# Two streams of other work beside a recurrent scan, on one Trainium2 core

## The chip, the cores and the metric

The kernel runs on one core of a Trainium2 chip. The core has a matrix engine (TensorE, in the profile PE, with PEld for its weight loads), VectorE (DVE), ScalarE (ACT), GpSimd (POOL) and SyncE (SP), which mostly issues transfers. Each engine works through its own queue in order. The metric is the device time of one execution in microseconds. The time before is 11773.53 us, the median of 3 runs (11760.24 to 11794.41).

## The reference, cut to what matters

The model is four layers on four images of 96 channels and 64 x 64 pixels.

```python
# layer 0: norms, 3x3 convolution, then a selective scan in four directions k over 4096 pixels,
#          192 channels x 16 states, then output norm, gate and projection
def step(h, inp):
    d_t, u_t, b_t, c_t = inp
    dA = jnp.exp(d_t[..., None] * A)                             # the decay, da
    h = dA * h + (d_t * u_t)[..., None] * b_t[:, :, None, :]      # inflow db, recurrence hh
    y = jnp.einsum('bkdn,bkn->bkd', h, c_t)                       # hc, then summed over the states
    return (h, y)
...
x = x + _L0_conv_ref(_gn(x), ...)      # layer 0
x = x + _L1_conv_ref(_gn(x), ...)      # layer 1: deformable 3x3 convolution: 9 gathered samples a pixel
t = t + _L2_attn_ref(_ln_t(t), ...)    # layers 2-3, on tokens: a Fourier block,
t = t + _L2_ffn_ref(_ln_t(t), ...)     #   a feed-forward block with fp8 rounding,
t = t + _L3_attn_ref(_ln_t(t), ...)    #   linear attention,
t = t + _L3_ffn_ref(_ln_t(t), ...)     #   and another feed-forward block
```

Images are independent of each other. Within an image the layers follow each other.

## The kernel before

The scan of layer 0 is cut into 1536 units: 4 images x 4 directions x 4 stretches of 1024 pixels x 24 groups of 8 channels with 16 states each, which fill 128 rows. A unit is a pipeline over the engines (loads of `da`, `du` and others in `fetch`, then one stage for each engine):

```python
def fetch(self, u, before):                     # cut
    u.da = sp.tile([128, T], F32, name=f"da{u.key}", tag="da", bufs=5)
    nc.sync.dma_start(u.da, src.unsqueeze(0).to_broadcast([NS, D8, T]))
def decay(self, u):    # ScalarE
    nc.scalar.activation(u.da, u.da, AF.Exp, scale=self.al[:, a : a + 1])
def inflow(self, u):   # TensorE: two matmuls into PSUM, db
def recur(self, u):    # VectorE
    nc.vector.tensor_mul(u.db, u.db, u.bc[:, 0, :])
    nc.vector.tensor_tensor_scan(hh, da, db, first, ALU.mult, ALU.add)
def weigh(self, u):    # GpSimd
    u.hc = self.sp.tile([128, T], F32, name=f"hc{u.key}", tag="hc", bufs=4)
    nc.gpsimd.tensor_mul(u.hc, u.hh, u.bc[:, 1, :])
def total(self, u, v): # TensorE sums hc over the states into py; settle (ScalarE) and store (SyncE) follow
```

All other work is a generator that yields its steps with an estimated cost on each of four engines. Between two units the kernel takes steps until one engine's share of a unit is spent. A pause costs nothing, and there is one stream only:

```python
SHARE = cost(5.0, 1.9, 4.5, 3.3)       # PE, DVE, ACT, POOL: us of other work per unit

def others():
    yield from l0.before(0)            # preparation of image 0
    for b in range(B):
        if b:
            yield from l1.image(b - 1)
        if b + 1 < B:
            yield from l0.before(b + 1)
        if b:
            yield from l23.image(b - 1)
        yield from l0.behind(b)        # output projection
    yield from l1.image(B - 1)
    yield from l23.image(B - 1)
...
for _, goes in l0.scan():
    if not goes:
        next(work)
        continue
    room = [min(r + s, SAVED * s) for r, s in zip(room, SHARE)]
    while min(room) > 0:
        step = next(work, None)
        if step is None:
            break
        room = [r - s for r, s in zip(room, step)]
```

The weighted sums of layer 1, for 128 pixels, run in three pieces of three taps:

```python
for k0 in (0, 3, 6):
    nc.vector.tensor_mul(g4, g4, w4.unsqueeze(2).to_broadcast([128, 12, C]))
    nc.vector.tensor_add(s1, s1, g[:, ks, 2 * C :])
    nc.vector.tensor_add(s2, s1[:, :, :C], s1[:, :, C:])
```

Of the kernel before, what the change touches and what calls it, by code (L numbers as in the profile page):

```python
# [20 lines left out]
L = H * W  # L21
# [21 lines left out]
def prepare(x, **w):  # L43
# [84 lines left out]
    a["selb"] = np.broadcast_to(eye8[:, :, None], (8, 8, 128)).copy()  # L128
# [37 lines left out]
SHARE = cost(5.0, 1.9, 4.5, 3.3)  # L166
SAVED = 1.5

# [28 lines left out]
def pause(rounds):  # L197
    for _ in range(rounds):
        yield NOTHING


class Net:
# [3 lines left out]
    def __init__(self, ctx, tc, ins):  # L206
# [5 lines left out]
        for name in ("vecs", "ident", "cen96", "grp3", "selv", "selb"):  # L212
            setattr(self, name, self.load(name, self.const))
# [7 lines left out]
        nc.vector.memset(self.one, 1.0)  # L221
        self.exp_and_log()

# [99 lines left out]
    def spread(self, rstd, j, n, key):  # L323

        k = rstd.shape[0]
        pb = self.mm(f"lnb{key}_{j}", n)
        self.nc.tensor.matmul(pb, lhsT=self.selb[:k, j, :n], rhs=rstd, start=True, stop=True)
        return pb
# [24 lines left out]
class Layer0:  # L353
# [45 lines left out]
    def before(self, b):  # L399
        net = self.net  # L400
        tc, nc, ins = net.tc, net.nc, net.ins
        with tc.tile_pool(name=f"l0u{b}", bufs=1) as up:
# [3 lines left out]
            with tc.tile_pool(name=f"l0b{b}", bufs=1) as sm:  # L406
# [4 lines left out]
                order = [(0, j) for j in range(NT)] + [(1, j) for j in reversed(range(NT))]  # L411
                xdbl = {}

                def chains():
                    yield self.projected(b, *order[0], us, xp_a, xp_c, sm, xdbl)
                    for n, (pr, j) in enumerate(order):
                        for t in range(3):
                            yield self.steps(b, pr, j, t, us, dtw, sm, xdbl)
                            if t == 0 and n + 1 < len(order):
                                yield self.projected(b, *order[n + 1], us, xp_a, xp_c, sm, xdbl)  # L420
# [3 lines left out]
    def inputs(self, b, up, us):  # L424

        net = self.net
        tc, nc, ins = net.tc, net.nc, net.ins
# [3 lines left out]
        with tc.tile_pool(name=f"l0a{b}", bufs=1) as big, tc.tile_pool(name=f"l0i{b}", bufs=2) as sm:  # L431
            x = big.tile([C, L], F32, name=f"xg{b}", tag="t1")
            nc.sync.dma_start(x, ins["x"][b])
            wc = big.tile([C, 9, 256], F32, name=f"wc{b}", tag="wc")
            nc.sync.dma_start(wc, self.wc_d)
            wz = big.tile([C, DI], F32, name=f"wz{b}", tag="wz")
            nc.sync.dma_start(wz, ins["w_in"][:, 256:])
            pad = big.tile([C, PW, PW], F32, name=f"pad{b}", tag="pad")
            for edge in (pad[:, 0, :], pad[:, PW - 1, :], pad[:, :, 0], pad[:, :, PW - 1]):
                nc.gpsimd.memset(edge, 0.0)  # L440
# [14 lines left out]
            def rows(j):  # L455
                return pad[:, 1 + j * NR : 1 + (j + 1) * NR, 1 : 1 + W]

            def as_rows(t):
                return t.rearrange("p (h w) -> p h w", w=W)

            yield from net.centred(x, cen, lambda j: (rows(j), as_rows), f"0_{b}", sm, bias)
            rs = net.rstd

            def normed_rows(j):
                pb = net.spread(rs, j, C, f"0_{b}")
                yield cost(pe=0.9)
                nc.vector.tensor_mul(rows(j), rows(j), as_rows(pb))
                yield cost(dve=0.7)
                nc.scalar.activation(
                    rows(j), rows(j), AF.Identity, scale=net.vec(V_ING, C), bias=net.vec(V_INB, C)  # L470
                )
                yield cost(act=0.8)

            yield from pipe((normed_rows(j) for j in range(NCH)), 3)
            xct_v = xc.rearrange("p (w h) -> p h w", h=H)

            def convolved(j):
# [28 lines left out]
                for g, (c0, n) in enumerate(((0, 128), (128, D2))):  # L506
                    pz = net.mm(f"pz{g}_{b}_{j}", n)
                    nc.tensor.matmul(pz, lhsT=wz[:, c0 : c0 + n], rhs=rows(j), start=True, stop=True)
# [11 lines left out]
            yield from pipe((convolved(j) for j in range(NCH)), 2, every=7)  # L520

    def projected(self, b, pr, j, us, xp_a, xp_c, sm, xdbl):
# [3 lines left out]
        nc = net.nc  # L526
        for q in range(2):
            k = 2 * pr + q
            xd = sm.tile([NX, T], F32, name=f"xd{b}_{k}_{j}", tag=f"xd{q}", bufs=2)
            hp = slice(64 * q, 64 * q + 64)  # L530
            for h in range(T // CH):
                t0 = j * T + h * CH
                ua = us[0][:, t0 : t0 + CH] if q == 0 else us[1][:, t0 // H : (t0 + CH) // H, :]
                px = net.mm(f"px{b}_{k}_{j}{h}", NX)
                nc.tensor.matmul(px, lhsT=xp_a[:, k, :], rhs=ua, start=True, stop=False)
                nc.tensor.matmul(
                    px, lhsT=xp_c[hp, pr, :], rhs=us[2][hp, t0 : t0 + CH], start=False, stop=True
                )
                nc.scalar.activation(xd[:, h * CH : (h + 1) * CH], px, AF.Identity, bias=net.vec(V_X1, NX))  # L539
                yield cost(pe=1.7, act=0.7)  # L540
            xdbl[pr, j, q] = xd
        for q in range(2):
            nc.sync.dma_start(
                self.bc_d[b][2 * pr + q][:, j * T : (j + 1) * T], xdbl[pr, j, q][: 2 * NS]
            )
        yield NOTHING

    def steps(self, b, pr, j, t, us, dtw, sm, xdbl):
# [3 lines left out]
        ts = slice(j * T, (j + 1) * T)  # L552
        tk = f"{b}_{pr}_{j}_{t}"

        def tile_of(name, bufs):
            return sm.tile([128, T], F32, name=f"{name}{tk}", tag=name, bufs=bufs)



        rl, ex = tile_of("rl", 2), tile_of("ex", 3)  # L560
        for h in range(T // CH):
            hs = slice(h * CH, (h + 1) * CH)
            pd = net.mm(f"pd{tk}_{h}")
            for q in (0, 1) if t == 2 else (t,):
                o, m = (pd[64 * q : 64 * q + 64], slice(128, DI)) if t == 2 else (pd, slice(0, 128))
                nc.tensor.matmul(  # L566
                    o,
                    lhsT=dtw[2 * NS :, 2 * pr + q, m],
                    rhs=xdbl[pr, j, q][2 * NS :, hs],
                    start=True,  # L570
                    stop=True,
                )
            nc.scalar.activation(rl[:, hs], pd, AF.Relu)
            nc.scalar.activation(ex[:, hs], pd, AF.Abs)
            yield cost(pe=1.9 if t == 2 else 0.95, act=1.2)
        nc.scalar.activation(ex, ex, AF.Exp, scale=-1.0)
        lw, w1 = tile_of("lw", 2), tile_of("w1", 2)
        nc.scalar.activation(lw, ex, AF.Ln, bias=net.one)  # L578
        nc.scalar.activation(w1, ex, AF.Identity, bias=net.one)
        yield cost(act=3.3)  # L580
        nc.vector.tensor_add(rl, rl, lw)  # L581
        nc.vector.scalar_tensor_tensor(w1, w1, -1.0, ex, ALU.add, ALU.subtract)
        yield cost(dve=3.2)
        nc.vector.tensor_sub(rl, rl, w1)  # L584
        yield cost(dve=1.3)
        if t == 1:
            u = us[1][:, j * T // H : (j + 1) * T // H, :]
            nc.gpsimd.tensor_mul(
                ex.rearrange("p (w h) -> p w h", h=H), rl.rearrange("p (w h) -> p w h", h=H), u
            )  # L590
        else:
            nc.gpsimd.tensor_mul(ex, rl, us[t][:, ts])  # L592
        parts = ((0, 128, 2 * pr + t, 0),) if t < 2 else ((0, 64, 2 * pr, 128), (64, 128, 2 * pr + 1, 128))
        for p0, p1, k, c0 in parts:
            nc.sync.dma_start(self.de_d[b][k][c0 : c0 + p1 - p0, ts], rl[p0:p1])
        yield cost(pool=2.4)
        du = sm.tile([128, 3, T], BF16, name=f"du{tk}", tag="du", bufs=2)
        nc.scalar.copy(du[:, 0, :], ex)
        yield cost(act=1.1)
        nc.gpsimd.tensor_sub(ex, ex, du[:, 0, :])  # L600
        yield cost(pool=2.4)
        nc.scalar.copy(du[:, 1, :], ex)
        yield cost(act=1.1)
        nc.vector.tensor_sub(du[:, 2, :], ex, du[:, 1, :])
        yield cost(dve=1.6)
        for p0, p1, k, c0 in parts:
            dst = self.du_d[b][k][:, c0 : c0 + p1 - p0, ts]
# [5 lines left out]
    def scan(self):  # L613
# [13 lines left out]
        for n in range(len(units) + 5):  # L627
            while loaded < min(n + ahead + 1, len(units)):
                u = units[loaded]
                while (u.b, u.k // 2, u.j) not in self.ready:  # L630
                    yield u.b, False
# [28 lines left out]
            yield at(min(n, len(units) - 1)).b, True  # L660
# [776 lines left out]
```

## Time and profile before

| | kernel before |
|---|---|
| time, median of 3 | 11773.53 us |
| head, to the first recurrence | 460 us |
| scan, first to last recurrence | 10002 us |
| tail | 1281 us |
| VectorE busy in the scan | 7575 us, so 2427 us idle |
| granted TensorE clock, mean | 0.672 |

The prediction below shows the busy line, the stages and several groups. Two further views matter for the comparison. The first is VectorE's row of the page's 40 slices, where each digit is the busy share in tenths, 9 being 90% or more:

```profile
DVE  0484888877997587754799668675489977534411
```

The second lists what ended VectorE's idle time within the scan (460 to 10462 us). In lists of waits, after the colon stand the total in us, the number of waits and the longest.

```profile
DVE db L716 <- PE db L705: 1160.7, 175, 34.0
DVE du L604 <- ACT du L602: 149.2, 43, 8.5
...
DVE nw L259 <- ACT nw L257: 114.5, 7, 20.3
...
DVE rl L581 <- ACT lw L578: 65.9, 43, 3.8
```

The 4s, 5s and 6s in the middle of the row lie in the scan, which VectorE should carry. Nearly half of the idle time there is one wait: 175 times the multiply `db` stood for a matmul that came late, by 6.6 us on average and by up to 34.0 us. TensorE was busy for 6359.67 of the scan's 10002 us, so it was not short of time on the whole. The longest of these waits, which ends at 5383 us, can be followed in the trace: TensorE stood 25.5 us in front of a matmul of output projection that waited for GpSimd's `ya`, and the matmul for `db` lay behind it in the same queue. The other waits were not followed one by one.

### The profile page before, as it was taken

What the parts mean: (1) busy time and instruction counts of PE and PEld (TensorE: products, weight loads), DVE (VectorE), ACT (ScalarE), POOL (GpSimd) and SP (SyncE); (2) the same over time, 40 slices, a digit from 0 to 9 for tenths busy, and PEclk for the clock granted to TensorE, in tenths of its full rate; (3) what the DMA queues carried; (4) which work ended last, traced back from release to release, by engine and by line L of the source; (5) the groups of instructions that cost most, each with busy time, mean ns of one, the idle gap of its engine ahead of it and who ended that gap; (6) DMA issues with size and microseconds to landing.
All of it is one profiled execution on the core that took longest, in us unless ns stands there. A gap on an engine that the chain in (4) does not pass through costs nothing. (4 is left out here: it accounts for less than half of the span.)

```text
span 11743.4 us, 86182 instructions
## 1 busy us (share of the span) xinstructions
PE 7376.3 (63%) x28728; PEld 2510.8 (21%) x28728; DVE 7989.7 (68%) x5552; ACT 4209.3 (36%) x6446; POOL 6050.7 (52%) x3212
## 2 busy tenths in 40 slices
PE   4758655565445866876554676687654468754486
PEld 1102000011111202521111120352111135212262
DVE  0484888877997587754799668675489977534411
ACT  2555543332222653343222365334322223431123
POOL 0362665655885464434688446443468844345601
PEclk9657655566555856876655675686665578766685
DMA  1354557766665455634666555552476656334410
GB/s 37 113 167 110 168 165 183 178 152 157 172 177 130 136 169 144 162 81 128 160 173 177 126 140 163 144 154 78 124 176 177 179 139 159 87 100 115 120 41 6
DMA packets 618302, 1605.21 MB, mean 137 GB/s; under 512 B 142185, under 2 KB 159165, under 8 KB 614978
## 3 DMA queue, kind: packets, MB, share of 16 engines
q1 hardware_dynamic: 544130, 1373.13, 44.4%
q0 software_dynamic: 73728, 226.57, 7.1%
q8 instruction: 229, 3.75, 0.1%
q14 instruction: 215, 1.76, 0.1%
HBM read 1343.11 MB, written 256.29 MB: 136 GB/s over the span
## 5 line engine op out<-in xcount | busy, mean ns | idle before, releaser
L730 POOL TENSOR_TENSOR hc<-hh,bc 128x1024 f32<-128x1024 f32 x1536 | 3927.2, 2557 | 3536.2 <-DVE hh L719 3053.3
L719 DVE TENSOR_TENSOR_SCAN hh<-da,st,db 128x1024 f32<-128x1024 f32 x1152 | 2703.5, 2347 | 194.6 <-ACT st L726 53.6
L705 PE MATMUL db<-du,rep 96*128 96x512 bf16 x3072 | 1356.7, 537 | 2136.8 <-DVE hh L719 1965.8
L716 DVE TENSOR_TENSOR db<-db,bc 128x1024 f32<-128x1024 f32 x1536 | 1872.2, 1219 | 1178.4 <-PE db L705 1178.3
L700 ACT ACTIVATE da<-da,w_al 128x1024 f32<-128x1024 f32 x1536 | 1758.0, 1149 | 1154.5 <-DMA da<-de 1091.4
L1018 POOL DMA_INDIRECT g<-table,idx x1152 | 1312.9, 1140 | 401.0 <-issue 352.4
L747 PE MATMUL py<-hc,w_fold 128*32 128x512 f32 x6144 | 1290.8, 915 | 15.2 <-POOL hc L730 15.2
L705 PEld LDWEIGHTS <-rep 96*128 96x128 bf16 x3072 | 238.9, 111 | 3346.3 <-DVE hh L719 2690.9
L719 DVE TENSOR_TENSOR_SCAN hh<-da,db 128x1024 f32<-128x1024 f32 x384 | 878.2, 2287 | 74.7 <-ACT da L700 20.6
L1046 PE MATMUL ps<-w_ident,s 128*96 128x128 f32 x1152 | 298.0, 390 | 985.9 <-DVE s L1042 981.6
L1047 ACT COPY st<-ps 96x384 f32<-96x384 f32 x384 | 182.2, 475 | 1853.2 <-PE ps L1046 1764.5
L1037 DVE TENSOR_TENSOR g<-g,wt 128x1152 f32<-128x1152 f32 x384 | 533.0, 1388 | 152.8 <-DMA g<-table,idx 152.8
L726 ACT COPY st<-hh 128x1 f32<-128x1 f32 x1152 | 212.0, 184 | 926.4 <-DVE hh L719 922.3
L484 PE MATMUL pc<-pad,wc 96*128 96x512 f32 x1152 | 516.2, 603 | 0.4
L1042 DVE TENSOR_TENSOR s<-g 128x288 f32<-128x288 f32 x384 | 438.0, 1141 | 18.8
L1046 PEld LDWEIGHTS ps<-w_ident,s 128*96 128x96 f32 x1152 | 156.8, 170 | 1326.4 <-issue 681.8
L1040 DVE TENSOR_TENSOR g<-g 128x576 f32<-128x576 f32 x384 | 394.8, 1028 | 5.8
L1053 PE MATMUL pd<-st,wdc 96*96 96x256 f32 x1152 | 397.9, 511 | 0.0
L581 DVE TENSOR_TENSOR rl<-rl,lw 128x1024 f32<-128x1024 f32 x96 | 221.8, 2311 | 244.3 <-ACT lw L578 243.3
L566 PE MATMUL pd<-xd,dtw 7*64 7x512 f32 (+1 forms) x512 | 315.0, 929 | 1.6 <-ACT xd L539 0.9
L747 PEld LDWEIGHTS py<-hc,w_fold 128*32 128x32 f32 x6144 | 171.2, 136 | 639.5 <-issue 564.7
L592 POOL TENSOR_TENSOR ex<-rl,xa 128x1024 f32<-128x1024 f32 x32 | 78.7, 2459 | 434.1 <-DVE rl L584 434.1
(240 smaller groups left out, 9776.0 us busy)
## 6 DMA issues: line engine op xcount, KB each, us to landing
da<-de SPq DMA_DIRECT2D x1536, 512.0 KB
du<-du SPq DMA_DIRECT2D x384, 192.0 KB
bc<-bcd SPq DMA_DIRECT2D x128, 512.0 KB
du<-du SPq DMA_DIRECT2D x64, 768.0 KB
y<-yb SPq DMA_DIRECT2D x384, 128.0 KB
de<-rl SPq DMA_DIRECT2D x64, 512.0 KB
m<-in_dft SPq DMA_DIRECT2D x128, 256.0 KB
du<-du SPq DMA_DIRECT2D x64, 384.0 KB
```

Source lines behind the costliest of these rows:

```text
L484: nc.tensor.matmul(pp, lhsT=wc[:, q, g * 128 : (g + 1) * 128], rhs=pad[:, r0 + dy : r0 + dy + NR, dx : dx + W], start=(q == 0), stop=(q == 8),
L700: self.net.nc.scalar.activation(u.da, u.da, AF.Exp, scale=self.al[:, a : a + 1])
L705: self.net.nc.tensor.matmul(db[:, h, :], lhsT=self.rep[:96, u.s % 4, :], rhs=u.du[u.s // 4][:, h * CH : (h + 1) * CH], start=True, stop=True,)
L716: nc.vector.tensor_mul(u.db, u.db, u.bc[:, 0, :])
L719: nc.vector.tensor_tensor_scan(u.along(u.hh), u.along(u.da), u.along(u.db), first, ALU.mult, ALU.add)
L730: self.net.nc.gpsimd.tensor_mul(u.hc, u.hh, u.bc[:, 1, :])
L747: nc.tensor.matmul(py[p0 : p0 + 32], lhsT=self.fold[:, u.i, :], rhs=hc[:, h * CH : (h + 1) * CH], start=u.add is None and u.i == 0, stop=( ...
L1018: nc.gpsimd.indirect_dma_start(out=g[:, k, :], out_offset=None, in_=self.tables[b % 2], in_offset=bass.IndirectOffsetOnAxis(ap=idx[:, 9 * ...
L1037: nc.vector.tensor_mul(g4, g4, w4.unsqueeze(2).to_broadcast([128, 12, C]))
L1042: nc.vector.tensor_add(s2, s1[:, :, :C], s1[:, :, C:])
L1046: nc.tensor.transpose(pt[:, k, :], s2[:, k, :], net.ident)
L1053: nc.tensor.matmul(po, lhsT=wdc[:, k, :], rhs=st[:, k, :], start=(k == 0), stop=(k == 8))
```

## The change

The intent is to run two streams of other work beside the scan instead of one after the other. One has preparation of all images and layers 2-3, the other has output projection and layer 1. Each stream earns a number of steps per unit, and pauses cost whole units, so the chains are spread. Room for the second stream is made by smaller pieces and fewer buffers. The scan's loads move from SyncE's queue to ScalarE's. The core of the diff, with cuts marked:

```diff
-SHARE = cost(5.0, 1.9, 4.5, 3.3)
+SHARE = cost(4.5, 2.0, 3.6, 3.0)
+LAG = tuple(0.5 * s for s in SHARE)
...
-def pause(rounds):
-    for _ in range(rounds):
-        yield NOTHING
+def pause(units):
+    for _ in range(units):
+        yield SHARE
...
# steps of preparation: half tiles (128 x 512), lw and w1 in one buffer, one operation moved to GpSimd
-        rl, ex = tile_of("rl", 2), tile_of("ex", 3)
...
-        lw, w1 = tile_of("lw", 2), tile_of("w1", 2)
+        lw, w1 = tile_of("lw", 1), tile_of("w1", 1)
...
-        nc.vector.scalar_tensor_tensor(w1, w1, -1.0, ex, ALU.add, ALU.subtract)
+        nc.vector.scalar_tensor_tensor(rl, pd, 0.0, lw, ALU.max, ALU.add)
+        nc.gpsimd.tensor_sub(w1, w1, ex)
...
# fetch: bc, du, add, da
-                nc.sync.dma_start(...)
+                nc.scalar.dma_start(...)
...
-        u.hc = self.sp.tile([128, T], F32, name=f"hc{u.key}", tag="hc", bufs=4)
+        u.hc = self.sp.tile([128, T], F32, name=f"hc{u.key}", tag="hc", bufs=3)
...
# output projection: blocks of two tiles instead of four, half of y at a time, fewer load buffers
-        HB = 4
+        HB = 2
...
# layer 1: whole-tile sums, two gather buffers
-                g = gp.tile([128, 9, 4 * C], F32, name=f"g{key}", tag="g", bufs=3)
+                g = gp.tile([128, 9, 4 * C], F32, name=f"g{key}", tag="g", bufs=2)
...
-                for k0 in (0, 3, 6):
...
+                nc.vector.tensor_mul(g4, g4, w4.unsqueeze(2).to_broadcast([128, 36, C]))
+                yield cost(dve=4.0)
...
-        def others():
...
+        def ends():
+            yield from l0.before(0)
+            l23 = Layers23(ctx, net, x2, out)
+            yield from l23.prepare()          # was in the head
+            yield from l0.before(1)
+            yield from l0.before(2)
+            yield from l0.before(3)
+            for b in range(B):
+                yield from l23.image(b)
+
+        def middle():
+            yield from l1.cleared()           # was in the head
+            for b in range(B):
+                yield from l0.behind(b)
+                yield from l1.image(b)
+
+        streams = [Stream(ends(), 2.6), Stream(middle(), 1.9)]
...
+            for stream in streams:
+                stream.credit = min(stream.credit + stream.earns, 3.0)
+            while go():                       # takes steps while there is credit and room
+                pass
+        while not all(stream.over for stream in streams):     # after the scan: alternately
```

## The prediction

> **What bounds the kernel now.** A scan of 1536 units is the spine: each unit is one multiply (`db`) and one recurrence (`hh`) on VectorE, one decay on ScalarE, one multiply on GpSimd. All other work (preparation of an image "before" its scan, output projection "behind" it, layer 1, layers 2-3) is emitted between units into the same in-order queues. I first read the page's busy line, then split the span where `hh` starts and ends: it runs from 460.0 to 10462.4 us. So: head 460, scan 10002, tail 1281 us. Next I cut these into stages by busy time per stretch.
>
> ```profile
> PE 7376.3 (63%) x28728; PEld 2510.8 (21%) x28728; DVE 7989.7 (68%) x5552; ACT 4209.3 (36%) x6446; POOL 6050.7 (52%) x3212
> ```
> ```profile
> core 0: us, PE busy (x) PEld busy (x) DVE busy (x) ACT busy (x) POOL busy (x), PEclk, DMA share, GB/s
> 0.00:156.00 156.00, 0.00 (x0) 0.00 (x0) 11.82 (x40) 4.41 (x10) 0.79 (x8) 1.00 0.19 53
> ...
> 1758.00:2313.00 555.00, 292.77 (x1008) 39.89 (x1008) 496.85 (x289) 190.00 (x280) 339.56 (x144) 0.56 0.73 183
> ...
> 2900.00:3513.00 613.00, 299.67 (x1026) 103.07 (x1026) 594.50 (x408) 150.31 (x249) 502.18 (x301) 0.58 0.66 174
> ...
> 5129.00:5568.00 439.00, 300.70 (x717) 78.62 (x716) 219.06 (x183) 158.47 (x290) 170.67 (x101) 0.67 0.41 108
> 10462.00:11107.00 645.00, 290.36 (x868) 136.84 (x864) 278.00 (x352) 82.50 (x162) 365.80 (x318) 0.65 0.42 114
> 11107.00:11743.00 636.00, 469.40 (x3028) 268.84 (x3028) 85.47 (x121) 179.25 (x334) 39.34 (x34) 0.70 0.09 25
> ```
> The same stretches for `hh` alone give the units in each (the count beside DVE):
> ```profile
> 1758.00:2313.00 555.00, 334.94 (x145) 21.69 (x118) 339.56 (x144) 0.56 0.73 183
> 2900.00:3513.00 613.00, 223.91 (x97) 13.42 (x72) 271.02 (x96) 0.58 0.66 174
> ...
> 5129.00:5568.00 439.00, 111.61 (x49) 8.64 (x47) 110.32 (x47) 0.67 0.41 108
> ```
> Three regimes. In 1758-2313 nothing runs beside the scan, and a unit costs 555/145 = 3.83 us, near VectorE's own 1.22 + 2.33 = 3.55. In 2900-3513 (layer 1's sampling) VectorE is 97% busy at 613/97 = 6.3 us. In 5129-5568 (end of layers 2-3, then output projection of image 1) a unit costs 439/49 = 9.0 us with no engine above 70%: that is waiting. It comes from chains emitted too densely and from SyncE's queue:
> ```profile
> SPq L696 <- DVE hh L719: 5594.0, 1128, 22.9
> ```
> ```profile
> DVE db L716 <- PE db L705: 104.7, 13, 34.0
> ...
> POOL ya L803 <- DMA ya<-y: 55.6, 5, 25.8
> ```
> The first line (the DMA queue's own waits, whole span) says SyncE stands half the span in the wait of the scan's `da` load for a scan to free its buffer; every other load queues behind it. The other two (chain of waits, 5129-5568): a late `ya` load stops GpSimd, then TensorE, whose in-order queue then brings `db` up to 34 us late to VectorE. VectorE's busy time within the scan is 7989.7 - 50.9 (head) - 363.5 (tail) = 7575 us of 10002, so 2427 us of the scan is VectorE idle.
>
> **What the Trainium skill says.** "SBUF — State Buffer", Who interferes with whom: a VectorE instruction with two SBUF inputs contends with a GpSimd instruction that reads SBUF, and the later one blocks fully. The trace agrees: the sum `s<-g` costs three times as much beside the scan (2900-3513) as in the tail (10700-11000), while the recurrence, with one SBUF and one PSUM input, never moves from 2347 ns.
> ```profile
> L1042 DVE TENSOR_TENSOR s<-g 128x288 f32<-128x288 f32 x68 | 94.5, 1390 | 2.4
> ```
> ```profile
> L1042 DVE TENSOR_TENSOR s<-g 128x288 f32<-128x288 f32 x67 | 30.7, 458 | 6.2
> ```
> "DMA: Bandwidth & Descriptors", Issuing engines are not separate DMA queues: transfers issued from different engines share the 16 DMA engines, and only the issuer's sequencer time is saved. So I expect no bandwidth from ScalarE's queue; what it buys is that other loads no longer stand behind a wait. An issue is not free:
> ```profile
> L696 SPq DMA_DIRECT2D da<-de x1536: 514/515/4586, 443.7 to 10444.4; - x192
> L581 DVE TENSOR_TENSOR rl<-rl,lw x96: 1210/2433/3429, 395.2 to 7375.9; 128x1024 f32<-128x1024 f32 x96
> ```
>
> **The change part by part.**
>
> *Head.* Before, table clearing holds SyncE from 16.5 to 113.6 us (16 stores, about 6 us apart), then weights of layers 2-3 are prepared until 156; only then the first group norm starts, and 304 us later the scan. Both now run beside the scan. I estimate the first image loaded by about 30 us, so 30 + 304 = 335: saves 125.
>
> *VectorE in the scan.* Sampling: per tile three times (1388 + 1028 + 1141) = 10.7 us become one triple over all nine taps. Uncontended cost (tail stretch) is 3 x (1356 + 758 + 458) = 7.7; three waits for the shared port, not nine, about 0.45 each on average: 9.0. Over the 96 tiles in the scan: -160 us. Preparation: four two-tile 128x1024 operations of 2311 + 1775 + 1799 + 1917 ns, 24 per image, = 187 us, become 48 x (0.70 reading PSUM + 1.15 + 1.15) = 144; one went to GpSimd (48 x 1.25). Over four images -170. Half of output projection moves from tail into the scan, three quarters of layers 2-3 of image 2 move the other way (-65). I get about 7290 us for the scan's VectorE, 4.75 us a unit.
>
> *ScalarE.* 1536 + 384 + 288 + 128 = 2336 issues at about 0.55 us: +1280 us, 0.84 a unit. With decay (1.15), state copy and other work I count 3.0 to 5.5 us a unit: below VectorE except in preparation, where they are close. The issue waits for `hh` of the unit before, which the state copy just after it did anyway.
>
> *Order and pace.* This is the main part. The queues' order shows, by unit: preparation of image 0 to unit 95, of 1 at 120-243, 2 at 251-382, 3 at 390-608; layer 1 of image 0 at 412-715; then per image output projection over 70 units (was 13), sampling over 209 (was 134), layers 2-3 over 303 beside them. The 150 units that ran alone are filled. To price it, I summed for every 24 units what stands in each queue, each kind at its mean from this trace, and took the larger of VectorE and TensorE:
> units 0-96: 4.85 us a unit; 96-168: 5.38; 168-264: 5.14; 264-288 (convolution, TensorE): 7.16; 288-408: 5.14; 408-456 (TensorE): 6.56; 456-720: 5.23; 720-912: 4.60; 912-1104: 5.18; 1104-1296: 4.60; 1296-1488: 5.18; to 1536: 5.28. Sum 7837.
> The same sum over the kernel before gives 8677 where 10002 were measured: a factor 1.153, which is 1.04 in sampling, 1.06 in the bare scan, and 1.3 to 1.46 where output projection or the end of layers 2-3 was squeezed into a dozen units. Those squeezed stretches are gone, since a pause now costs whole units and a stream takes 2.6 or 1.9 steps a unit. I choose 1.15 for the preparation stretch (2449 us of the sum, ScalarE near its limit) and 1.09 for the rest (5388): 2816 + 5873 = 8690.
>
> *Tail.* Before: 645 for output projection and layer 1 of image 3, 636 for layers 2-3. At the end of the scan the new order still has one and a half halves of the Fourier block and the rest of layers 2-3 of image 2 (about 500 us alone). It goes step for step beside layer 1 of image 3, but its last block spills over (about 60). TensorE has some 240 + 265 us there in alternating order, so I take 720 instead of 645 (less one half of output projection, more mutual waiting). 720 + 60 + 640 = 1420, a loss of 140.
>
> Sum: 335 + 8690 + 1420 = 10445, say 10450.
>
> **Rivals.**
> 1. DMA becomes the bound. Its engines' share is 51.6% of the span, of which some 5650 us fall in the scan; in 8690 that is 65%, and the bare scan ran at 73% share and 183 GB/s with ScalarE waiting for `da` 98 times (296.6 us). For: output projection now reads half columns in 128-byte pieces. Against: VectorE was 90% busy at that share. If bursts at block starts hurt: scan 9200, total 11000.
> 2. ScalarE's queue becomes the clock: a late decay delays the next issue, which delays the next decay. For: 4.8-5.5 us a unit in preparation. Against: it has two units between issue and need. It would cost 0.5 us on 600 units, 300 us: 10750.
> 3. Three PSUM buffers and two gather buffers shared by two streams tie them together, TensorE waits for an eviction and `db` comes late as before. Then the factor stays 1.15: scan 9035, total 10800.
> 4. Smoothing works fully (factor 1.05): 8230, total 9950.
> 5. The spilled layers 2-3 simply add to the tail: 1700, total 10700.
>
> **Range and chances.** The scan's factor dominates: 1.05 to 1.18 is 8230 to 9250, and the tail adds +-120. Range 9900 to 11100. Being within 2% of 11774 needs a scan above 9780, a factor of 1.25, which only the squeezed stretches had. Faster 0.93, same 0.05, slower 0.02.
>
> **What will show it.** First `hh` near 335; last near 9030; tail near 1420 with sampling stretched. No stretch of bare scan at 3.8 us before unit 1500; units at 5.2-5.6 us in sampling with VectorE over 90%; VectorE's idle time waiting for `db` well below the 1178 us of before; `ya` no longer late. Wrong would be: ScalarE idle on `da` above 1500 us, VectorE below 80% in units 456-1488, or a DMA share above 80%.

## The result

The changed kernel takes 10492.59 us, the median of 4 runs (10462.69 to 10508.04). The kernel before took 11783.97 us in the same rounds. The ratio is 0.8903, with a 95% interval of 0.8877 to 0.8929. A ratio here is the mean time of one kernel's runs over the mean of the other's in the same rounds, so it is not quite the ratio of the medians quoted. Executions over 1.5% slower than the fastest of the same kernel are left out of the means. Where kernels of different rounds are compared below, I take the difference of their ratios times 11,770 us.

| | before | predicted | after |
|---|---|---|---|
| time | 11773.53 | 10450 | 10492.59 |
| head | 460 | 335 | 323 |
| scan | 10002 | 8690 | 8676 |
| of it units 0-456 | | 2816 | 2853 |
| of it units 456-1536 | | 5873 | 5823 |
| tail | 1281 | 1420 | 1462 |
| VectorE busy in the scan | 7575 | 7290 | 7201 |
| VectorE idle in the scan | 2427 | | 1475 |
| granted TensorE clock, mean | 0.672 | | 0.702 |

The busy line of the changed kernel's page and its row for VectorE:

```profile
PE 7119.7 (68%) x28728; PEld 2481.0 (24%) x28728; DVE 7640.0 (73%) x4993; ACT 4352.7 (42%) x6950; POOL 6456.3 (62%) x3603
...
DVE  0788688587759999987878889788888897444211
```

The stages of the changed kernel, by busy time in each stretch:

```profile
core 0: us, PE busy (x) PEld busy (x) DVE busy (x) ACT busy (x) POOL busy (x), PEclk, DMA share, GB/s
0.00:323.00 323.00, 229.84 (x422) 75.50 (x422) 41.48 (x61) 145.34 (x175) 26.44 (x29) 0.88 0.22 62
323.00:3153.00 2830.00, 2029.64 (x5220) 447.99 (x5220) 2117.23 (x1475) 1604.91 (x2400) 1685.63 (x933) 0.68 0.61 160
3153.00:4650.00 1497.00, 804.41 (x2654) 199.79 (x2654) 1405.94 (x804) 586.57 (x939) 1228.27 (x693) 0.64 0.70 183
4650.00:5616.00 966.00, 742.01 (x4242) 324.10 (x4243) 789.50 (x521) 356.52 (x580) 554.62 (x268) 0.75 0.72 177
5616.00:6685.00 1069.00, 653.88 (x2311) 214.89 (x2309) 944.49 (x548) 393.76 (x668) 891.55 (x483) 0.68 0.68 174
8999.00:10461.00 1462.00, 1055.68 (x6192) 609.15 (x6188) 397.52 (x367) 412.72 (x787) 474.00 (x376) 0.73 0.25 69
```

The bare stretch at 3.8 us a unit is gone, and so are the squeezed ones at 9. The fastest 48 units take 4.20 us each, the slowest 7.01. In 3153-4650 (sampling of image 0, 268 units at 5.59 us) VectorE is 94% busy, and in 5616-6685 (sampling of image 1 beside layers 2-3, 192 units at 5.57 us) 88%. In the preparation stretch, 323-3153, it is 75% busy, so waits are left there. The granted clock rose as well; whether as a cause or as a consequence, no run tells.

VectorE's waits within the scan (323 to 8999 us), and two of SyncE's own waits over the whole span:

```profile
DVE db L741 <- PE db L730: 574.4, 178, 22.0
DVE rl L604 <- ACT lw L599: 137.4, 57, 17.3
DVE g L1085 <- DMA g<-table,idx: 85.3, 35, 6.7
```
```profile
SPq L789 <- ACT yb L782: 1976.3, 130, 33.4
...
SPq L619 <- DVE rl L607: 984.8, 180, 18.3
```

The wait of `db` for its matmul has halved, 1160.7 to 574.4 us, at nearly the same number of waits: each became shorter. That is 586 of the 952 us that VectorE's idle time fell by. SyncE no longer stands in front of the loads of `da`, but it now stands in front of the store of `y` (L789) and of the store of `de` (L619) instead.

The rows that answer to those of the sums, of preparation's first operation and of the `da` load:

```profile
L1085 DVE TENSOR_TENSOR g<-g,wt 128x3456 f32<-128x3456 f32 x128 | 593.1, 4634 | 148.6 <-DMA g<-table,idx 147.3 <-issue 1.2
...
L1088 DVE TENSOR_TENSOR g<-g 128x1728 f32<-128x1728 f32 x128 | 261.4, 2042 | 1.0
...
L1091 DVE TENSOR_TENSOR s<-g 128x864 f32<-128x864 f32 x128 | 153.3, 1197 | 1.7
L604 DVE SCALAR_TENSOR_TENSOR rl<-pd,lw 128x512 f32<-128x512 f32 x192 | 130.7, 681 | 309.6 <-ACT lw L599 309.5
```
```profile
L721 ACTq DMA_DIRECT2D da<-de x1536: 521/522/1621, 306.4 to 8973.7; - x192
```

The three sums of a tile are now (593.1 + 261.4 + 153.3) / 128 = 7.87 us, against 10.67 before, as a mean over all 128 tiles. For the 96 tiles within the scan it is 8.21 against 11.65. The prediction expected 9.0 for these, coming from 10.7, which is the mean over all tiles.

### The profile page after: what moved, and what is told of

It reads as the page before. It is cut to its first block, busy times and chain, and to the rows that moved or that the text cites. A ratio compares the mean times of both kernels' runs of the same rounds, so it can differ in the third digit from the quotient of the medians.

```text
span 10460.6 us, 85850 instructions
## 1 busy us (share of the span) xinstructions
PE 7119.7 (68%) x28728; PEld 2481.0 (24%) x28728; DVE 7640.0 (73%) x4993; ACT 4352.7 (42%) x6950; POOL 6456.3 (62%) x3603
## 5 line engine op out<-in xcount | busy, mean ns | idle before, releaser
L755 POOL TENSOR_TENSOR hc<-hh,bc 128x1024 f32<-128x1024 f32 x1536 | 3885.8, 2531 | 1937.3 <-DVE hh L744 1003.6
L725 ACT ACTIVATE da<-da,w_al 128x1024 f32<-128x1024 f32 x1536 | 1762.6, 1149 | 3126.4 <-DMA da<-de 981.5
L730 PE MATMUL db<-du,rep 96*128 96x512 bf16 x3072 | 1293.0, 515 | 2324.6 <-DVE hh L744 2147.1
L1074 POOL DMA_INDIRECT g<-table,idx x1152 | 1449.7, 1258 | 417.2 <-issue 191.1
L1085 DVE TENSOR_TENSOR g<-g,wt 128x3456 f32<-128x3456 f32 x128 | 593.1, 4634 | 148.6 <-DMA g<-table,idx 147.3
L605 POOL TENSOR_TENSOR w<-w,ex 128x512 f32<-128x512 f32 x192 | 259.0, 1349 | 650.7 <-ACT w L601 648.9
L607 DVE TENSOR_TENSOR rl<-rl,w 128x512 f32<-128x512 f32 x192 | 304.9, 1588 | 95.6 <-POOL w L605 95.3
L1332 POOL CAST xqf<-fl 96x512 fp8e5<-96x512 f32 x64 | 51.5, 810 | 496.6 <-DVE fl L1291 496.5
L604 DVE SCALAR_TENSOR_TENSOR rl<-pd,lw 128x512 f32<-128x512 f32 x192 | 130.7, 681 | 309.6 <-ACT lw L599 309.5
L592 PE MATMUL pd<-xd,dtw 7*128 7x512 f32 (+1 forms) x512 | 324.5, 953 | 43.9 <-ACT xd L570 28.5
L1109 PE MATMUL pd<-st,wdc 96*96 96x256 f32 x1152 | 309.0, 414 | 0.0
L518 PEld LDWEIGHTS pc<-pad,wc 96*128 96x128 f32 x1152 | 220.5, 195 | 310.5 <-issue 290.4
L628 DVE TENSOR_TENSOR du<-ex,du 128x512 bf16<-128x512 f32 x192 | 234.6, 1222 | 79.7 <-ACT du L626 75.3
```

What stands on the lines that cost most here:

```text
L518: nc.tensor.matmul(pp, lhsT=wc[:, q, g * 128 : (g + 1) * 128], rhs=pad[:, r0 + dy : r0 + dy + NR, dx : dx + W], start=(q == 0), stop=(q == 8),
L592: nc.tensor.matmul(o, lhsT=dtw[2 * NS :, 2 * pr + q, m], rhs=xdbl[pr, j, q][2 * NS :], start=True, stop=True)
L607: nc.vector.tensor_sub(rl, rl, w1)
L725: self.net.nc.scalar.activation(u.da, u.da, AF.Exp, scale=self.al[:, a : a + 1])
L730: self.net.nc.tensor.matmul(db[:, h, :], lhsT=self.rep[:96, u.s % 4, :], rhs=u.du[u.s // 4][:, h * CH : (h + 1) * CH], start=True, stop=True,)
L755: self.net.nc.gpsimd.tensor_mul(u.hc, u.hh, u.bc[:, 1, :])
```

## The experiments

A prediction that comes out right can still be right for wrong reasons. The theory on test was: (a) the order and the pace are the main part, (b) the smaller VectorE work is a second one, (c) the head a third, and (d) ScalarE's queue frees other loads. The rivals are that one of the smaller parts carries the gain, or that a wait introduced by the change holds more back.

All twelve kernels gave correct results. The changed kernel has 0.8903 in this list.

| run | what it is | us, median | ratio to before, 95% | head / scan / tail |
|---|---|---|---|---|
| e1_loads_sync | after, loads in SyncE's queue | 10476.46 | 0.8895 (0.8880-0.8910) | 323 / 8580 / 1580 |
| e2_before_loads_act | before, loads in ScalarE's queue | 11784.67 | 1.0012 (0.9995-1.0028) | 458 / 10031 / 1283 |
| e3_old_order | after, one stream, old order and pace | 12084.14 | 1.0261 (1.0243-1.0278) | 323 / 10096 / 1658 |
| e4_free_pauses | after, pauses free | 10688.0 | 0.9076 (0.9058-0.9094) | 323 / 8941 / 1431 |
| e9_old_share | after, pauses free, old share | 10746.92 | 0.9130 (0.9107-0.9153) | 323 / 8976 / 1444 |
| e5_hc4 | after, fourth hc buffer | 10503.36 | 0.8924 (0.8905-0.8944) | 323 / 8714 / 1480 |
| e6_middle24 | after, second stream at 2.4 | 10629.72 | 0.9033 (0.9017-0.9050) | 321 / 8878 / 1429 |
| e7_sample_thirds | after, sums in thirds | 10492.58 | 0.8921 (0.8905-0.8937) | 322 / 8772 / 1404 |
| e8_head | after, two tasks back in the head | 10593.0 | 0.9002 (0.8986-0.9018) | 436 / 8649 / 1519 |
| e10_ends22 | after, first stream at 2.2 | 10490.76 | 0.8925 (0.8899-0.8950) | 322 / 8643 / 1512 |
| e11_ends21_mid23 | after, streams at 2.1 and 2.3 | 10651.62 | 0.9056 (0.9040-0.9072) | 324 / 8849 / 1476 |
| e12_before_buffers | before, with fewer buffers | 11577.09 | 0.9861 (0.9838-0.9884) | 459 / 9824 / 1297 |

### Which queue issues the scan's loads

```diff
 # e1: the changed kernel, all four loads of fetch (bc, du, add, da)
-        nc.scalar.dma_start(u.da, ...)
+        nc.sync.dma_start(u.da, ...)
```

> The changed kernel with the scan's loads issued by SyncE again. My theory (the order of work is the main gain, ScalarE's queue a smaller one, because other loads no longer stand behind the scan's wait): 10,600 to 10,850 us, with the loss in units where output projection or preparation load (0-400 and 720-800), and `ya` late again. Rival (the queue is the main gain): 11,300 us or more. Rival (the queue buys nothing, because the 2336 issues cost ScalarE what they free on SyncE): within 1% of 10,493.

```diff
 # e2: the kernel before, the same four loads
-        nc.sync.dma_start(u.da, ...)
+        nc.scalar.dma_start(u.da, ...)
```

> The kernel before with only the scan's loads moved to ScalarE's queue. My theory: 11,480 to 11,680 us, a gain of 100 to 300, since the squeezed stretches stay squeezed. Rival (the queue is the main gain): below 10,900. Rival (the queue buys nothing): within 1% of 11,784.

My theory fell in both. In the old order the move changes nothing (1.0012, and the interval includes 1). In the new order, moving the loads back doesn't change the total either: the ratios' intervals overlap. In the profiled runs the scan was 96 us shorter and the tail 118 us longer, so two opposite effects may hide behind the unchanged total; they rest on one profile each, and no cause was found. `ya`, which was to come late again, did not: GpSimd's wait for it is 148.7 us before, 51.5 in the changed kernel, 68.3 in e1, and in e2, with `da` out of SyncE's queue, still 131.0. SyncE's own waits show why the move may be worth nothing. First e1, then e2, whole span:

```profile
SPq L721 <- DVE hh L744: 3576.5, 886, 16.6
```
```profile
SPq L764 <- ACT yb L757: 2743.6, 165, 63.4
```

When the loads are in SyncE's queue, it stands in the wait for a scan to free the `da` buffer. Taken out of there, it stands in the next wait, that of the `y` store for its result. The seven longest of SyncE's waits add up to some 5,750 us in e1 and 7,000 us in e2, over half of the span in either place. In e2 VectorE still waited 1134.8 us for `db`, against 1178.3 before, so the late matmuls did not come from SyncE's waits for `da`. The Trainium skill's "DMA: Bandwidth & Descriptors", Issuing engines are not separate DMA queues, says that only the issuer's sequencer time is saved. Here not even that time counted in the total: 2336 issues, those of `da` at 522 ns each, went to another engine, and the total stayed.

### The order and the pace

The changed kernel with the old order in one stream, free pauses and the old share:

```diff
-        streams = [Stream(ends(), 2.6), Stream(middle(), 1.9)]
+        streams = [Stream(one(), 100.0)]       # one(): the old others(), no limit on credit
-SHARE = cost(4.5, 2.0, 3.6, 3.0)
+SHARE = cost(5.0, 1.9, 4.5, 3.3)
-        yield SHARE                            # in pause; LAG likewise
+        yield NOTHING
```

> The changed kernel with the order and pace undone: one stream in the order of before, pauses that cost nothing, the shares of before; short head, ScalarE's queue and the new VectorE operations stay. My theory: about 11,150 us (11,000 to 11,400): 11,784 less 137 for the head, less some 300 of VectorE work, less 100 to 300 for the queue; a bare stretch of some 150 units at 3.8 us each returns, and stretches of 8 us a unit or more in output projection. Rival (the queue or the VectorE operations carry the gain): 10,800 or less.

It is not only slower than the changed kernel. It is 2.6% slower than the kernel before. The bare stretch is back (3.82 and 3.70 us a unit in units 192-288), and squeezed ones too (10.12, 9.90 and 10.11 us a unit at three places). So the order and pace are worth (1.0261 - 0.8903) x 11,770 = 1598 us, more than the whole gain. In the profiled runs 1420 us of it lie in the scan and 196 in the tail. Under the old order the rest of the change costs some 300 us; where they lie is taken up in the last experiment. VectorE's waits in its scan:

```profile
DVE db L741 <- PE db L730: 780.5, 146, 29.6
DVE nw L278 <- ACT nw L276: 360.3, 12, 49.0
DVE g L1085 <- DMA g<-table,idx: 272.6, 81, 9.1
DVE rl L604 <- ACT lw L599: 219.0, 122, 21.1
```

Against the kernel before, `db` waits less, but VectorE now waits for the reciprocal square root `nw` (114.5 before), for preparation's logarithm `lw` (65.9 before) and for the gather.

Two runs split the 1598 us. The first makes only the pauses free, the second also restores the old share:

```diff
-        yield SHARE            # pause
-            yield LAG          # four places
+        yield NOTHING
+            yield NOTHING
```

> The changed kernel, both streams, but a pause or a lag after a load costs nothing again, so that fewer units pass between a load and its use. My theory: the paid pauses are part of the gain, 10,550 to 10,800 us, with waits on `m<-in_dft` and `ya<-y` longer than in the changed kernel. Rival (two streams alone do it; a pause only delays work): 10,493 or less, since layers 2-3 of image 2 get further before the scan ends.

```diff
 # as above, and
-SHARE = cost(4.5, 2.0, 3.6, 3.0)
+SHARE = cost(5.0, 1.9, 4.5, 3.3)
```

> The changed kernel with free pauses (as in the run with free pauses, 10688 us) and also the old share of work per unit (5.0, 1.9, 4.5, 3.3 instead of 4.5, 2.0, 3.6, 3.0): what is left of the change in order is the two streams with their rates. With one stream in the old order and the same share and pauses it was 12084 us. Theory A (the two streams side by side are the main part, the pace the small one): 10,650-10,850 us, so that the streams are worth 1,230-1,430 us, with a scan of 8,900-9,100 us and a tail under 1,430. Rival (the smaller share is what spreads the squeezed stretches): 11,100-11,600 us.

The times are those of my theory in e4 and of Theory A in e9 (whose tail, 1444, is a little over the 1,430 expected). From the ratios: two streams with their rates in place of one, 1.0261 to 0.9130, are worth 1331 us. The smaller share, 0.9130 to 0.9076, is worth 64 us. Pauses that cost units, 0.9076 to 0.8903, are worth 204 us. The reason given for e4 did not hold: the waits on `m<-in_dft` and `ya<-y` within the scan are 23.0 and 42.0 us, against 21.6 and 38.0 in the changed kernel. Of the 265 us that e4's scan is longer, 181 lie in its first 456 units, and the wait of `db` is 665.5 instead of 574.4 us. So what the pauses did was to thin out the dense preparation stretch.

The step of 1331 us holds three things at once: two chains are taken alternately, the order is new (all preparation first, and layers 2-3 beside output projection and layer 1), and each stream is limited to 2.6 or 1.9 steps a unit. e9 still has this limit and e3 has none. No run gave one stream a limit, or two streams none, so which of the three carries the 1331 us is not shown.

### The head

```diff
 # the clearing of the tables and the preparation of weights, in front of the first image
+            yield from l1.cleared()
+            l23 = Layers23(ctx, net, x2, out)
+            yield from l23.prepare()
             yield from l0.before(0)
```

> The changed kernel with the clearing of the tables and the preparation of the weights of layers 2-3 in front of the first image again, as before. Theory A (this part of the change is worth what it takes off the head, 125-137 us, less what the same work costs beside the scan, 20-50 us): first recurrence near 450-460 us, scan 20-50 us shorter, total 10,570-10,610 us. Rival (beside the scan the work costs as much as in the head, or the head is bound by something else): within 40 us of the changed kernel, 10,450-10,530 us.

Theory A held for the total and the scan. The first recurrence starts at 436 instead of 323 us, somewhat before the expected 450, the scan is 26 us shorter, and by the ratios the part is worth (0.9002 - 0.8903) x 11,770 = 117 us. The tail is 57 us longer, which the theory did not have; the order beside the scan shifts too, since the second stream starts earlier. The prediction had 125 from the head alone, with nothing for the cost beside the scan.

### VectorE's sums

```diff
-                nc.vector.tensor_mul(g4, g4, w4.unsqueeze(2).to_broadcast([128, 36, C]))
...
+                for k0 in (0, 3, 6):
+                    nc.vector.tensor_mul(g4, g4, w4.unsqueeze(2).to_broadcast([128, 12, C]))
...
```

> The changed kernel with layer 1's weighted sums in three pieces of three taps again, as before. In the kernel before those sums held VectorE for 1383.4 us, in the changed one for 1033.9 us. Theory A (VectorE bounds the sampling stretches, so its time counts one for one): 250-350 us longer, 10,740-10,840 us. Rival 1 (VectorE is idle for 1475 us of the scan and the pieces slip into it): 10,440-10,560 us. Rival 2 (shorter operations hold the shared port less long each time and the recurrence runs smoother): faster than 10,440 us.

The time is that of Rival 1, 10492.58 us, although VectorE's work grew. (The expectation's 1383.4 and 1033.9 us stand in no view; the rows of the two traces add up to 1365.8 and 1007.8.) Over the whole span its sums took 629.6 + 350.6 + 295.5 = 1275.7 us instead of 1007.8, and VectorE was 203.7 us busier in all (7843.7 against 7640.0). The comparison isn't pure, since other step costs also shift the order: layers 2-3 of image 2 start about 70 units earlier, the scan is 96 us longer and the tail 57 us shorter. So Rival 1's reason, that the pieces slip into idle time, is not shown. What can be said is that the wide sums as built here bring nothing that can be measured, and the prediction's step that took 160 us of VectorE work off the scan's time is not supported.

### A fourth buffer for hc

The changed kernel showed a wait that the kernel before hardly had: GpSimd stood 780.0 us for the matmul that frees `hc`.

```diff
-        u.hc = self.sp.tile(..., tag="hc", bufs=3)
+        u.hc = self.sp.tile(..., tag="hc", bufs=4)
-                nw = op.tile(..., tag="nw", bufs=1)
+                nw = op.tile(..., tag="xo", bufs=1)       # room
-                    xr = op.tile(..., tag="xr")
+                    xr = op.tile(..., tag="xr", bufs=1)   # room
```

> The changed kernel with a fourth buffer for GpSimd's product (hc); the room comes from two small tiles of output projection that share one buffer. In the changed kernel GpSimd stood 780.0 us (147 times) waiting for the matmul that frees hc, a wait the kernel before hardly had. Theory A (those waits hold GpSimd, and through it the state sums and the next images, up): the wait falls below 300 us and the time to 10,250-10,400 us. Rival (GpSimd is 62% busy and waits for a TensorE that is late for other reasons; VectorE sets the pace): the wait falls, the time stays within 0.5% of the changed kernel, 10,440-10,540 us. I lean to the rival.

The rival held. In e5's row for GpSimd's product the wait for `py` is 35.1 us instead of 780.0:

```profile
L755 POOL TENSOR_TENSOR hc<-hh,bc 128x1024 f32<-128x1024 f32 x1536 | 3872.8, 2522 | 1894.8 <-DVE hh L744 1577.6 <-issue 103.4 <-PE py L772 35.1
```

The idle time before it is nearly the same as in the changed kernel, 1894.8 against 1937.3 us: GpSimd now waits for the recurrence instead (1577.6 against 1003.6). A large wait on an engine that has slack is not a cost.

### The rates of the streams

```diff
-        streams = [Stream(ends(), 2.6), Stream(middle(), 1.9)]
+        streams = [Stream(ends(), 2.6), Stream(middle(), 2.4)]     # e6
+        streams = [Stream(ends(), 2.2), Stream(middle(), 1.9)]     # e10
+        streams = [Stream(ends(), 2.1), Stream(middle(), 2.3)]     # e11
```

> The changed kernel with the second stream (output projection and layer 1) earning 2.4 instead of 1.9 steps a unit. Layer 1 of each image ends some 50 units earlier, so layers 2-3 of image 2 start in about unit 1445 instead of 1498 and less of them is left after the scan. Theory A (the scan had slack to take them up, and the tail's loss comes from the stream's low rate): tail 1300-1380 instead of 1462, scan within 40 us of 8676, total 10,360-10,460 us. Rival (a denser stream brings back waits, as in the kernel before): tail shorter but scan longer by over 100 us, total 10,500-10,650 us.

> The changed kernel with the first stream (preparation, layers 2-3) earning 2.2 instead of 2.6 steps a unit; preparation of image 3 ends in unit 638 instead of 603, long before unit 1152 needs it, and layers 2-3 are about as spread as before. Theory A (density in the preparation stretch costs waits, so a slower stream smooths it): the first 456 units take 2,740-2,800 us instead of 2,830 and the total is 10,380-10,460 us. Rival (the work is only moved to later units): within 0.5% of the changed kernel, 10,440-10,540 us. I lean to the rival.

> The changed kernel with the first stream at 2.1 and the second at 2.3 steps a unit: the sum of both rates stays (4.4 to 4.5 of before), but layer 1 ends some 30 units earlier, so layers 2-3 of image 2 start in unit 1465 instead of 1505. With the second at 2.4 and the first at 2.6 the time was 10630 us. Theory A (there the sum of the rates was too dense, not the second stream's own): scan within 40 us of 8676 and tail 1,390-1,440, total 10,380-10,480 us. Rival (the second stream's gathers and sums are what suffers from a faster pace, or from standing beside the wrong neighbours): 10,560-10,680 us.

In e6 the rival held, with the scan 202 us longer. VectorE's waits in its scan, the first two lines, show that `db` is no worse. The gather is: 226.0 instead of 85.3 us.

```profile
DVE db L741 <- PE db L730: 562.7, 189, 23.8
DVE g L1085 <- DMA g<-table,idx: 226.0, 57, 9.4
```

A pause of two empty steps lies between a tile's gather and its use. At a higher rate these steps go by in fewer units, while the gather takes as long as before. That the two are connected is read from this wait and was not tried by itself. The tail was only 33 us shorter, although layers 2-3 of image 2 had started earlier. Over e6's whole span VectorE waited 119.8 us for the table of base positions, once for 108.0:

```profile
DVE pos L1028 <- DMA w_base<-in_base: 119.8, 3, 108.0
```

In e6's scan this wait is only 11.8 us, so the 108 lie in the tail, in layer 1 of the last image. They cost nothing that can be seen there: the instruction that waited starts 195 us into the tail, and in the changed kernel 193. What keeps the tail long is that layer 1 of the last image ends 801 us into it, against 786 in the changed kernel. The earlier start could only save what was left over after that: layers 2-3 of the last image load their input 803 instead of 849 us into the tail.

e11 tells the two theories apart: with nearly the same sum of rates as the changed kernel, but a faster second stream, the time is 10651.62 us and the gather wait in its scan 180.7 us. A slower first stream alone (e10) costs nothing. So the sum of the rates is not what hurts; raising the second stream's rate is. Whether its own pace does it or the neighbours that its work then meets, which the rival also named, was not separated: the gather's wait grew by 141 us (e6) and 95 (e11), VectorE's idle time in the scan by 248 and 206. In e10 both the first half of Theory A and the rival came true: the first 456 units took 2749 us instead of 2853, and the total stayed (0.8925). The 104 us came back later, 71 in the rest of the scan and 50 in the tail, out of 1512 instead of 1462. Work moved out of a dense stretch is not saved.

### What the buffers cost

The last run asks where the 300 us of e3 come from: the buffers given up, or the smaller pieces.

```diff
 # the kernel before
-        lw, w1 = tile_of("lw", 2), tile_of("w1", 2)
+        lw, w1 = tile_of("lw", 1), tile_of("w1", 1)
-        ... tag="hc", bufs=4)          # and g 3, za and zc 3, xr 4, the sampling pool 2, two yt
+        ... tag="hc", bufs=3)          # and g 2, za and zc 2, xr 2, the sampling pool 1, one yt
```

> The kernel before with the buffers that the change gave up to make room for a second stream: one instead of two for lw and w1, two instead of three for the gather, three instead of four for hc, one set instead of two in the sampling pool, two instead of three or four for the loads of output projection, one yt. Its order is unchanged. The changed kernel put back into the old order had been 12084 us, some 300 us above the kernel before, and this is to tell where those 300 come from. Theory A (the buffers): 11,950-12,100 us, with VectorE's wait for the gather well above 153 us. Rival (the work in smaller pieces, above all output projection in blocks of two tiles, whose reciprocal square roots VectorE then waited for over 360.3 us of the scan instead of 114.5): 11,760-11,860 us. I lean to the rival.

Neither expectation held. With fewer buffers the kernel before is 1.4% faster, 11577.09 us, clear of the noise. The scan is 178 us shorter, and VectorE's work in it is 7405 instead of 7575 us, 170 us less for the same instructions, while its idle time stays (2418 and 2427 us). The saving comes from one row, whole span, first before and then e12:

```profile
L1042 DVE TENSOR_TENSOR s<-g 128x288 f32<-128x288 f32 x384 | 438.0, 1141 | 18.8
```
```profile
L1042 DVE TENSOR_TENSOR s<-g 128x288 f32<-128x288 f32 x384 | 214.5, 559 | 18.8
```

The last sum of each piece fell from 1141 to 559 ns (223.5 us in all), while the sum before it rose from 394.8 to 438.2 us. I sorted these 384 sums by what GpSimd did at the same time:

```
                                              before          e12
only issuing the gather (L1018)               262, 458 ns     278, 458 ns
issuing, and its product hc ran too (L730)    108, 2717 ns      9, 2718 ns
in hc only                                      9, 2478 ns      9, 2491 ns
idle                                            5, 458 ns      88, 458 ns
```

The sum of 458 ns is not slowed down by the gather's issue. When `hc` runs as well, the sum waits for it: in the trace before, each of these 117 sums ended 312 to 326 ns after its `hc`. In 90 of them the sum's record begins 7 to 151 ns before that of `hc`, and it was still the sum that waited. Before, 117 of 384 sums ran into it; in e12, 18. That one of the two waits for the other in full is the rule of the Trainium skill's "SBUF — State Buffer", Who interferes with whom, seen here in the trace of one row; which of them had come first, the records' start times don't tell. With fewer buffers GpSimd is stopped at other moments: in e12 it waits 1531.8 us for the matmul that frees `hc`, which the kernel before hardly did, and 128.6 us for a sum to free a gather buffer. Which of the two moves `hc` out of the sums' way was not separated.

So the buffers don't explain e3. Against e12, e3 is (1.0261 - 0.9861) x 11,770 = 471 us slower. The profiles show where its time lies: against the kernel before, e3's head is 137 us shorter, its scan 94 us longer and its tail 377 us longer. In the first 238 us of that tail the linear attention and feed-forward block of image 2 run, which the kernel before had finished within the scan. Then output projection of image 3 runs with all of its eight tiles, until 430 us; in the kernel before four were left, done by 74 us. So with the change's parts the old order gets less of the other work done beside the scan. Whether the smaller pieces, the half-size blocks of output projection, the step costs or another part of the change cause this, no run took apart. It stays open.

No tried version beats the changed kernel. e1 has the lowest median, 16 us lower, within the scatter.

## Why the prediction was right

**Total, head and scan.** The time came 43 us from the predicted 10450. The head was 323 against 335, the scan 8676 against 8690. The main step, the sum by 24 units of the larger of VectorE and TensorE times a factor, gave the right time: the factors measured are 2853 / 2449 = 1.165 in preparation (1.15 chosen) and 5823 / 5388 = 1.081 in the rest (1.09 chosen). That the scan came within 14 us is in part luck. The two errors, +37 and -50 us, nearly cancel, and the factors divide a measured time by predicted work, which had errors of its own (see below).

**Order and pace.** "This is the main part" is shown: e3 puts it at 1598 us. The prediction named "since a pause now costs whole units and a stream takes 2.6 or 1.9 steps a unit" as what removes the squeezed stretches. Its first half is the small part: paid pauses bring 204 us (e4), and without them no 48 units take over 7.5 us each. Its second half, the rates, was not tried apart from the two streams and their order; together these bring 1331 us.

**ScalarE's queue.** The step "what it buys is that other loads no longer stand behind a wait" failed. e1 and e2 show that it buys nothing in the total, in either order; `ya` stays late in e2 (131.0 us) and stays early in e1 (68.3). That SyncE's queue then stands in front of its next wait is the likely reason. The reading of 5594.0 us of SyncE's waiting as a cause of late loads was a mistake of the same kind as taking GpSimd's 780.0 us for a cost. Even in the instance that the prediction shows, the wait of 34.0 us, it does not fit: just before it issued that `ya` load at 5356 us, SyncE had waited 5.5 us for a result of layers 2-3 and 6.8 us for its store to `out` to land, and not for `da`. The prediction gave this no separate number, so the total did not suffer.

**VectorE in the scan.** 7201 us was measured where 7290 was predicted, again with errors that partly cancel. The sums of the 96 tiles in the scan saved 96 x (11.65 - 8.21) = 330 us, where 160 was predicted from the mean over all tiles. The three operations of preparation took 192 x (681 + 1588 + 1222) ns = 670 us instead of the 576 predicted. Four operations had taken 749 us before, so 79 us were saved, where 170 was predicted. e7, which has the changed kernel's buffers and the old width, takes 10.64 us a tile in the scan: of the 3.44 us saved, 2.43 go with the width and 1.01 with the rest of the change. But e7 is no slower, so this work did not count in the time, whereas in e12 a saving of 170 us of VectorE's work came with a scan 178 us shorter. Idle time alone does not tell which it will be: e12's kernel has more of it (2418 us) than the changed one (1475).

**ScalarE's cost.** The added 0.55 us an issue was right (522 ns) and did not show as a cost: ScalarE waited 981.5 us for `da` over the span, below the 1500 named as a sign of error. The DMA share in the scan is 0.67, close to what the first rival computed (65%), and the time it forecast for bursts, 11000, did not come.

**Tail.** 1462 against 1420. Of the three terms, 720 + 60 + 640, the trace shows 786 us to the end of layer 1, 63 from there until layers 2-3 of the last image load their input, and 613 for these. So the term that was too small is layer 1 beside the rest of layers 2-3. In e6 these layers start earlier and the tail is only 33 us shorter, while the scan is 202 us longer.

**Rivals and signs.** For the third, that shared PSUM and gather buffers tie the streams, the gather's waits at higher rates (e6, e11) speak, but no run changed these buffers under two streams; the factor stayed under 1.10 after preparation. The second, ScalarE as the clock, is not seen: VectorE waited only 37.6 us of the scan for a decay. The fourth, full smoothing at 9950, was not reached, and the fifth, a tail of 1700, did not come. Of the signs, VectorE was busy for 88% of units 456-1488 (wrong would have been below 80%), and in the second sampling stretch 88% where over 90% was named.

## What to carry to other kernels

When one engine carries a recurrence, try two limited streams of independent work beside it before tuning pauses, queues or buffers. Here the two streams, with their order and rates, were worth 1331 of 1598 us. A large total beside a wait shows where a queue stands and not what it costs: remove the wait in an experiment and see whether the next one takes its place, as it did here from the load of `da` to the store of `y`, and for `hc` from TensorE to the recurrence. Where the work is spread, the rate of each stream has to be tried by itself: here raising one stream's rate cost some 180 us even where the sum of the rates stayed (0.9056 against 0.8903).

## What the Trainium skill lacked or had wrong

- "SBUF — State Buffer", Who interferes with whom: it says that such a sum was not seen to stall a DMA's descriptor generation, and marks the reason as inferred. The traces agree for the sum's side: in e12, 278 sums beside a gather's issue took 458 ns, the same as the 88 with GpSimd idle. Whether the issue is held up was not looked at. It doesn't say how the lock looks in a profile: the mean of a row grows from 458 to 1141 ns because about one instruction in three waits for the end of GpSimd's (2717 ns in the mean for 108 of them), so a mean between the two is a share of collisions.
- No page that I read has it that fewer buffers can make a kernel faster: 11577.09 against 11752.35 us with the order unchanged, as GpSimd's `hc` met 18 instead of 117 of VectorE's last sums.
- "DMA: Bandwidth & Descriptors", Issuing engines are not separate DMA queues: no run here contradicts it. The section lacks a figure for what an issue costs on the issuing queue (here 522 ns on ScalarE, 1536 times for `da` alone), and a warning that the move can leave the total as it was (1.0012, and 0.8895 against 0.8903).
